# All row tiles of an attention block multiplied in pairs, with the steps of a batch written in a new order

## The chip, the cores and the metric

The kernel runs on one core of one Trainium2 chip. A core has a matrix engine (TensorE, in the profile PE, with its weight loads as PEld), three engines for elementwise work (VectorE or DVE, ScalarE or ACT, GpSimd or POOL) and SyncE (SP), which here only starts DMA transfers. Each engine runs its own list of instructions in the order in which the program wrote them, and waits where an instruction needs another engine's result. The metric is the time of one execution on the device in microseconds (us).

## The reference

The input x has 8 batches of 1024 rows by 256 columns, in float32. One block of a transformer is computed, with a modulation from a small vector c:

```python
mod = (_silu(L0_c) @ L0_wmod).reshape(L0_c.shape[0], 6, 1, -1)
sa, ca, ga, sb, cb, gb = (mod[:, 0], mod[:, 1], mod[:, 2], mod[:, 3], mod[:, 4], mod[:, 5])
...
h = _layernorm(x, axis=-1) * (1 + ca) + sa
x = x + ga * attn(h)      # scores (h*w_lhs)(h*w_rhs)^T, softmax over rows, times h
h = _layernorm(x, axis=-1) * (1 + cb) + sb
x = x + gb * ffn(h)       # relu(h W1 + b1) W2 + b2, inner width 1024
```

The gates ga and gb are first moved away from zero (at least 0.25 in size).

## The kernel before

**Tiles.** A batch has eight row tiles of 128 rows (NT = 8), in two halves g of four tiles (TH = 4, 512 rows). The main loop goes over batches b and tiles i; each pair (b, i) is a step. In step i of batch b the kernel computes the scores of tile i + 2 (`direct`, L412), works on the weights of tile i + 1 (called `late`), multiplies tile i's weights by the normalised x (`product`, `pair_begin`, `pair_end`), and does a part of the feed-forward work of batch b - 1. So attention of one batch runs beside the feed-forward part of the batch before. Batch 0 has no feed-forward part beside it and has its own loop body; `tail` (L1392) finishes the last batch's feed-forward work.

**Scores.** They are symmetric up to the column scales, so only columns at or right of the tile are computed; `mirror` (L433) transposes blocks on DVE, and `move` (L309) sends them through DRAM by SP (four writes D_m, one read) into the lower triangle. `row_max` (L469) takes a row's maximum on DVE, `max_turn` (L474) transposes it on PE into bank m, `subtract` (L479) and `exponent` (L491) make the weights pT.

**Products.** A full `product` (L501) is eight matmuls of 257 columns: 256 of x, scaled in the tile xg, and a column of ones that gives the sum. A pair of tiles can instead be multiplied by a scheme of seven half-size products (Strassen's, in Winograd's form) in place of eight. `pair_begin` (L547) makes two of them into the PSUM tile pp, ACT copies one to W, and `pair_begin_sum` (L566) adds them on DVE. `left_sums` (L575) makes four sums of weights on POOL; `right_sums` (L534) makes four of xg once per batch. `pair_end` (L587) makes the other five products into pq and pr, `pair_out` (L609) combines all on DVE and adds to x, `pair_stats` (L635) takes the statistics of the second layer norm. Before, tiles 0 and 5 use the full product and the pairs are (1,2), (3,4) and (6,7).

**Feed-forward.** It also uses seven products for eight. A step with i % 4 < 2 (`step_units`, L1186) does one unit of the first layer: products one and five (`unit_start`, L759, with the ACT copies k1 and k5), two, six (with the copy k2), three, seven and four (L774 to L821), in the banks A, B and E; relus follow on ACT, and `turn_first` and `turn_last` (L831, L839) make sums on POOL. Bank A takes products one, six, seven and four after one another, so each must wait until the result before it has been read. A step with i % 4 >= 2 (`step_rows`) does products of the second layer (`y_one` to `y_seven`, L850 to L887).  `y_gate` and `y_turn` scale the result and transpose it (T_y) through DRAM, `y_add` (L913) adds it to x on POOL and `y_out` writes x out.

**The next batch.** During batch b, each half of batch b + 1 goes through statistics (`prepare_stats`, DVE), `prepare_rstd` (ACT), `prepare_norm` (L281, four ACT instructions into xg), `prepare_blocks` (L340, transposes T_a on DVE, sent through DRAM to X_a), and `prepare_turn_apart` (L345), which scales X_a on ACT into the right and the left operand of the scores (two instructions each, L351). Additions and multiplications by rows (`x_plus`, `xg_times`) are put into a list, and `spare()` issues one of them on POOL at chosen places. The second layer norm goes through `ffn_rstd`, `ffn_norm`, `ffn_blocks` (T_f, X_f) and `ffn_turn` (hT on DVE and ACT, four sums hs on POOL).

**What sets the order.** The order is written out by hand, and `pin` (L72) holds every engine to it. Nothing is planned by costs. The step functions are the list of queues: a call writes its instructions into PE's, DVE's, ACT's, POOL's and SP's list at that place. PSUM has eight banks: two for scores (s), one each for m, A, B and E, two (o) for the products.

Of the kernel before, what the change touches and what calls it, by code (L numbers as in the profile page):

```python
# [24 lines left out]
def adaln_block_kernel(  # L25
# [158 lines left out]
    def columns(src, at):  # L184
        n = src.shape[0]
        pv = any_bank(f"pt_v{at}")
        nc.tensor.transpose(pv[:, :n], src, ident[:n, :n])
        nc.scalar.copy(cols[:, ds(at, n)], pv[:, :n])
# [398 lines left out]
    def pair_end(b, i, between=None):  # L587
# [5 lines left out]
        for n, (out, lhs, rhs) in enumerate((  # L593
# [6 lines left out]
            if between and n == 2:  # L600
                between()
# [385 lines left out]
    columns(wv, NI)  # L987
# [76 lines left out]
    def make_gcol():  # L1064
        pg = any_bank("pt_g")
        for j in range(2):
            for k in range(ND):
                nc.tensor.transpose(
                    pg[:, ts(j * ND + k, B)], rows_sb[:, 2 + j, ts(k, P)], ident[:B, :B]
                )  # L1070
        nc.scalar.copy(gcol.rearrange("p j k b -> p (j k b)"), pg[:, : 2 * ND * B])

# [32 lines left out]
    def make_columns():  # L1105
        make_gcol()
        columns(b1_rows, 0)
# [4 lines left out]
    def early(b, i):  # L1112

        if b == 0:

            if i in (1, 2):
                prepare_rstd(1, i - 1)
            elif i == 5:
                ffn_rstd(0, 0)
            if i in (1, 2):  # L1120
                prepare_norm(1, i - 1)
                x_plus(1, i - 1)
            if i in (3, 4):
                xg_times(1, i - 3)
            elif i == 5:
                prepare_turn(1, 0)
            elif i == 6:
                load_x(2, 0)
        else:
            if i == 2 and b + 1 < B:  # L1130
                prepare_norm(b + 1, 0)
            elif i == 6 and b + 2 < B:
                load_x(b + 2, 0)

    def turns(b, i):

        if b == 0 and i == 2:
# [4 lines left out]
        elif b == 0 and i == 3:  # L1142
            prepare_blocks(1, 1)
        if b > 0 and i == 2:
            ffn_turn(b - 1, 1)
        if i == (7 if b < B - 1 else 6):
            ffn_turn(b, 0)

    def middle(b, i):

        if i == 0:
            ffn_norm(b - 1, 1)
        elif i == (6 if b < B - 1 else 5):
            ffn_norm(b, 0)

    def norms(b, i):
        if b > 0 and i == 0:
            ffn_blocks(b - 1, 1)
        if b == 0:
            if i == 0:  # L1160
                prepare_start(1)
        elif b + 1 < B:
            if i == 1:
                prepare_start(b + 1)
                prepare_stats(b + 1, 0)
            elif i == 2:
                prepare_blocks(b + 1, 0)
                x_plus(b + 1, 0)
                xg_times(b + 1, 0)
        elif i == 5:  # L1170

            ffn_blocks(b, 0)
        if b == B - 1:
            return
        if i == 6:
            if b == 0:
                ffn_norm(b, 0)
            ffn_blocks(b, 0)
# [6 lines left out]

    def step_units(b, i, ahead, late, extra):  # L1186
        fb, fg, c = b - 1, i // TH, i % TH * 2
        ub, ug = (b - 1, 0) if i >= TH else (b - 2, 1)
        back = i % TH == 0 and ub >= 0
        more = b + 1 < B  # L1190
        main = {
            0: lambda n: product(b, 0, (n,)),
            1: lambda n: None,
            4: lambda n: None,
            5: lambda n: product(b, 5, (n,)),
        }[i]

        unit_start(fb, fg, c)
        if i == 0:
            ffn_rstd(b - 1, 1)  # L1200
        elif i == 4:
            y_gate(fb)
            if more:
                prepare_rstd(b + 1, 1)
        if ahead:
            mirror(*ahead)
        unit_two(c)
        if i == 4:
            y_turn(fb, 0)
        max_turn(*late)  # L1210
        unit_six(c)
        if i == 0 and back:
            for q in range(2):
                y_add(ub, ug, q)
        if i != 4:
            subtract(*late)
        if extra:
            exponent(*late)
        unit_three(c)
        if extra:  # L1220
            max_turn(*extra)
            unit_seven(c)
        if (b, i) == (B - 1, 5):
            ffn_rstd(b, 0)
        if i == 0 or (b, i) == (B - 1, 5):
            middle(b, i)
        if i == 1:
            exponent(*late)
            left_sum(b, i)
        elif i == 4 and more:  # L1230
            prepare_norm(b + 1, 1)
            x_plus(b + 1, 1)
        elif i == 5:
            exponent(*late)
            if more:
                prepare_turn_apart(b + 1, 1, 1)
        relu_left(c)
        if i == 0 and not extra:
            exponent(*late)
        if i == 1:  # L1240
            pair_begin(b, i, lambda: unit_seven(c))
        elif i == 4:
            pair_end(b, 3, lambda: unit_seven(c))
        else:
            main(0)
            if not extra:
                unit_seven(c)
            else:
                subtract(*extra)
        relu_right(c)  # L1250
        turn_first(c)
        if i == 5 and more:
            prepare_turn_apart(b + 1, 1, 0)
        if i == 4:
            if more:
                prepare_blocks(b + 1, 1)
                xg_times(b + 1, 1)
            weights(*late)
        main(1)
        unit_four(c)  # L1260
        if i == 1:
# [3 lines left out]
        if i == 4:  # L1265
            for q in range(2):
                y_add(ub, ug, q)
        if i in (0, 4):
            turn_last(c)
        turns(b, i)  # L1270
        norms(b, i)
        if extra:
            exponent(*extra)
        if i in (0, 5):
            product_out(b, i)
        elif i == 4:
            pair_out(b, 3)
            if b == B - 1:
                pair_stats(b, 3)
        if back:  # L1280
            y_out(ub, ug)

    def step_rows(b, i, ahead, late):
# [3 lines left out]
        if i == NT - 2:  # L1287
            for q in (1, 3):
                if (b, q) in two_t:
                    pair_stats(b, q)  # L1290
        if i == 2:
            left_sums(b, 1)
        if ending:
            pair_end(b, i - 1)
            pair_out(b, i - 1)
            pair_stats(b, i - 1)
        if i % TH == 2:
            if i == 6:
                max_turn(*late)
                weights(*late)  # L1300
                y_one(fb, fg)
            else:
                y_one(fb, fg)
                max_turn(*late)
            if ahead:
                mirror(*ahead)
            if i == 2:
                turn_last(2)
            y_two(fb, fg)
            if i == 2 and more:  # L1310
                prepare_rstd(b + 1, 0)
            elif i == 6 and more:
                ffn_rstd(b, 0)
            y_six()
            if i == 2:
                weights(*late)
            else:
                turn_last(2)
                pair_begin(b, i)
                left_sums(b, i)  # L1320
                pair_begin_sum(b, i)
        else:
            if i == 3:
                pair_begin(b, i, lambda: max_turn(*late))
            elif ahead:
                max_turn(*late)
            if ahead:
# [4 lines left out]
            if i == 3:  # L1332
                pair_begin_sum(b, i)
            if late:
                weights(*late)
            y_four(fb)
        spare()
        early(b, i)
# [205 lines left out]
```

## Time and profile before

| what | value |
|---|---|
| median of 3 runs | 780.77 us (780.23 to 780.78) |
| the profiled execution's own time | 780.81 us |
| its span in the profile | 779.0 us |
| DVE busy | 506.5 us (65%) |
| POOL busy | 473.7 us (61%) |
| ACT busy | 409.0 us (52%) |
| granted PE clock | full in all 40 slices |

A busy time is the time in which an engine executes instructions of the program; a matmul's end is modelled, so PE's starts tell more than its lengths. One `matmul` of the program in float32 makes two records, so a group of four matmuls shows as x8. A line of the timeline gives start, length, engine, the source line, the operation with output and input tiles, and in brackets the idle time before it and what ended it. Windows that are given without heading list the length, then busy time of PE, PEld, DVE, ACT and POOL with the number of instructions, the granted clock, the DMA share and GB/s.

### The profile page before, as it was taken

How to read it: one execution, taken by the hardware profiler on the slowest of the kernel's cores; microseconds unless marked ns; L12 is line 12 of the kernel's file. 1: busy time of each engine (PE TensorE's matmuls, PEld its weight loads, DVE VectorE, ACT ScalarE, POOL GpSimd, SP SyncE). 2: the span in 40 equal slices, each digit the busy share in tenths (PEclk: the TensorE clock that was granted, in tenths of full speed). 3: DMA queues.
4: the chain of work that ended last, by engine and by line, in shares of the span. 5: the costliest groups of instructions: out<-in, count | busy, mean ns of one | idle time of the engine just before them, and what ended most of it. 6: DMA issues, size and time to landing. Idle time of an engine off the chain costs nothing.

```text
span 779.0 us, 11552 instructions
## 1 busy us (share of the span) xinstructions
PE 757.4 (97%) x3876; PEld 624.4 (80%) x3876; DVE 506.5 (65%) x1075; ACT 409.0 (52%) x762; POOL 473.7 (61%) x481
## 2 busy tenths in 40 slices
PE   8999999999999999999999999999999999999998
PEld 4687788788987888778887888878888787988886
DVE  6787767576675767757667576766767576574421
ACT  4464637546474456645555455654637546262531
POOL 3753483866739577466766577566683866458320
PEclk9999999999999999999999999999999999999999
DMA  8033444265444543445533555335543354134220
GB/s 299 15 109 95 135 122 111 82 179 154 118 117 120 164 132 109 139 123 160 144 86 125 148 149 157 100 101 178 153 139 102 94 162 133 33 90 122 77 85 27
DMA packets 106210, 95.18 MB, mean 122 GB/s; under 512 B 29700, under 2 KB 98848, under 8 KB 106152
## 3 DMA queue, kind: packets, MB, share of 16 engines
q1 hardware_dynamic: 98408, 85.81, 38.2%
q10 hardware_dynamic: 7744, 8.65, 3.5%
q8 instruction: 30, 0.49, 0.3%
q14 instruction: 28, 0.23, 0.1%
HBM read 50.62 MB, written 43.81 MB: 121 GB/s over the span
## 4 chain that ended last, share of the span: by engine, by line
PE 76%; ACT 11%; DVE 6%; issue 5%; DMA 1%; DVEq 0%
PE psc L421 13%; PE pa L738 12%; PE ya L738 10%; PE po L509 9%; PE pe L738 6%; PE pr L603 5%; PE yc L738 5%; PE pp L557 4%; PE py L954 4%; PE pq L603 3%; PE pb L738 3%; ACT pT L492 2%; DVE pT L483 2%; PE yb L738 2%; ACT xg L290 2%
## 5 line engine op out<-in xcount | busy, mean ns | idle before, releaser
L421 PE MATMUL psc<-rT,lT 128*128 128x512 f32 (+3 forms) x384 | 134.7, 487 | 0.0
L421 PEld LDWEIGHTS psc<-rT,lT 128*128 128x128 f32 x384 | 68.2, 191 | 38.0 <-issue 27.0
L492 ACT ACTIVATE pT<-pT 128x1024 f32<-128x1024 f32 x64 | 67.7, 1058 | 58.1 <-DVE pT L483 58.1
L428 ACT COPY sc<-psc 128x512 f32<-128x512 f32 (+3 forms) x96 | 45.1, 476 | 90.7 <-PE psc L421 67.6
L483 DVE TENSOR_TENSOR pT<-sc,pm 128x1024 f32<-128x1024 f32 x64 | 77.3, 1207 | 9.4 <-PE pm L476 7.7
L509 PE MATMUL po<-xg,pT 128*128 128x257 f32 x352 | 82.9, 381 | 0.0
L836 POOL TENSOR_TENSOR ft<-f 128x512 f32<-128x512 f32 x28 | 35.7, 1274 | 74.4 <-ACT f L825 74.4
L471 DVE TENSOR_REDUCE m<-sc 128x1 f32<-128x1024 f32 x64 | 77.4, 1210 | 3.4 <-ACT sc L428 2.6
L738 PE MATMUL pa<-hT,w 128*128 128x256 f32 x256 | 67.5, 386 | 10.5 <-ACT f L817 9.9
L509 PEld LDWEIGHTS po<-xg,pT 128*128 128x128 f32 x352 | 66.3, 190 | 10.1 <-issue 0.7
L918 POOL TENSOR_TENSOR x<-x,Y 128x512 f32<-128x512 f32 x28 | 35.1, 1275 | 57.2 <-DMA Y<-D_y 57.2
L738 PEld LDWEIGHTS pa<-hT,w 128*128 128x128 f32 x256 | 46.8, 190 | 25.3 <-ACT f L817 13.4
L738 PE MATMUL pa<-hs,w1s 128*128 128x256 f32 x256 | 66.3, 381 | 0.1
L756 ACT COPY k<-pa 128x512 f32<-128x512 f32 x64 | 37.3, 583 | 47.7 <-PE pa L738 47.1
L444 DVE STREAM_TRANSPOSE Tm<-sc 128x896 f32<-128x896 f32 (+6 forms) x49 | 34.9, 711 | 32.1 <-ACT sc L428 31.8
L652 POOL TENSOR_TENSOR x<-x,rows 128x256 f32<-128x256 f32 x64 | 45.3, 740 | 14.7 <-ACT rows L1059 10.4
L738 PE MATMUL yc<-f,w2s 128*128 128x256 f32 x224 | 53.1, 380 | 0.9 <-DVE Y L877 0.9
L803 DVE SCALAR_TENSOR_TENSOR f<-pa,cols,k 128x256 f32<-128x256 f32 x64 | 28.0, 480 | 38.9 <-PE pa L738 38.9
L738 PE MATMUL ya<-ft,w 128*128 128x256 f32 x224 | 52.9, 380 | 0.0
L738 PEld LDWEIGHTS pa<-hs,w1s 128*128 128x128 f32 x256 | 45.4, 191 | 8.1 <-POOL pT L584 2.0
L573 POOL TENSOR_TENSOR s<-pT 128x512 f32<-128x512 f32 x21 | 26.7, 1273 | 40.9 <-ACT pT L492 36.5
L724 POOL TENSOR_TENSOR hs<-hT 128x256 f32<-128x256 f32 x16 | 11.6, 725 | 60.5 <-DVE hT L715 60.5
(161 smaller groups left out, 1743.9 us busy)
## 6 DMA issues: line engine op xcount, KB each, us to landing
D_f<-T_f SPq DMA_DIRECT2D x60, 128.0 KB, 2.4
X_f<-D_f SPq DMA_DIRECT2D x15, 512.0 KB, 3.9
D_a<-T_a SPq DMA_DIRECT2D x56, 128.0 KB, 2.3
D_y<-T_y SPq DMA_DIRECT2D x56, 128.0 KB, 3.2
Y<-D_y SPq DMA_DIRECT2D x14, 512.0 KB, 3.6
out_dram<-x SPq DMA_DIRECT2D x14, 512.0 KB, 4.0
X_a<-D_a SPq DMA_DIRECT2D x13, 512.0 KB, 3.4
x<-in_L_attn_x_dram ACTq DMA_DIRECT2D x12, 512.0 KB, 4.1
```

The lines of the kernel that those rows point to most:

```text
L421: nc.tensor.matmul(psc[:, : hi - lo], lhsT=lT_t[b, i // TH][:, k, ts(i % TH, P)], rhs=rT_t[b, n][:, k, lo - n * HALF : HALF], start=(k == ...
L428: nc.scalar.copy(score_row(b, i)[:, lo // V : hi // V, :], psc[:, : hi - lo].rearrange("p (n v) -> p n v", v=V),)
L471: nc.vector.tensor_reduce(m, score_row(b, i), AX.XY, ALU.max)
L483: nc.vector.tensor_tensor(pT.rearrange("p j (a v) -> p j a v", v=V), score_columns(b, i), pm[:, :P].rearrange("p (j a v) -> p j a v", j=1, ...
L492: nc.scalar.activation(pT_t[b, i], pT_t[b, i], AF.Exp)
L509: nc.tensor.matmul(po[:, : D + 1], lhsT=pT[:, t, :], rhs=xg_t[b][:, t, 0 : D + 1], start=(t == 0), stop=(t == NT - 1),)
L603: nc.tensor.matmul(out, lhsT=lhs[:, t, :], rhs=rhs[:, t, :], start=(t == 0), stop=(t == TH - 1),)
L652: queue.append(lambda: nc.gpsimd.tensor_tensor(out, in0, row, op))
L738: nc.tensor.matmul(out, lhsT=lhsT, rhs=rhs, start=first, stop=True, skip_group_check=True)
L756: nc.scalar.copy(k, src)
L836: add(ft[:, 0, c : c + 2], f22, f12, ALU.subtract)
L918: nc.gpsimd.tensor_tensor(x2, x2, y, ALU.add)
```

## The change

From batch 1 on every tile is in a pair: (0,1), (2,3), (4,5), (6,7). `pair_begin` is called in the even steps, `pair_end` in the odd ones. In steps 0, 1, 4 and 5 products of the unit stand between pair products: in an even step products seven and three stand between the two of `pair_begin`; in an odd step they stand after the first product of `pair_end`, and product four after the third. In steps 2 and 6 a y product stands between the two of `pair_begin`. Product four's relu is on DVE in steps 0 and 4 (with the exception of batch 1's step 0).

The steps are written in a new order. Among what moves: T_f of `ffn_blocks(b-1, 1)` from step 0 to 1; the load of the next batch's second half from step 2 to 1; the normalisation, T_a and additions of the next batch's second half from step 4 to 3, with `prepare_norm` between the two `prepare_turn_apart` of the first half; in step 2 the statistics of the pair and `ffn_turn` stand ahead of `row_max`; in step 7 `row_max` stands behind `y_turn` and `ffn_turn`; in step 6 `row_max` stands behind `ffn_norm`. In batch 0 only a helper changes: small columns are transposed into a bank that another transpose already uses.

```diff
-    def columns(src, at):
+    def columns(src, at, pv):
         n = src.shape[0]
-        pv = any_bank(f"pt_v{at}")
...
-            if between and n == 2:
-                between()
+            if n in between:
+                between[n]()
...
+        def sums():
+            unit_seven(c)
+            unit_three(c)
...
         max_turn(*late)
         unit_six(c)
+        subtract(*late)
         if i == 4:
             y_turn(fb, 0)
...
+        def after():
+            exponent(*late)
+            relu_left(c)
+            relu_right(c)
+            turn_first(c)
...
+        elif even:
+            pair_begin(b, i, sums)
             exponent(*late)
+            left_sums(b, i)
+            relu_left(c)
+            if i == 0:
+                ffn_norm(b - 1, 1)
+            relu_right(c)
+            turn_first(c)
+            unit_four(c, True)
+        elif i == 1:
+            pair_end(b, i - 1, {1: sums, 3: lambda: (after(), unit_four(c))})
+            if more:
+                prepare_start(b + 1)
+                prepare_stats(b + 1, 0)
+        else:
...
+            spares(4)
+            pair_end(b, i - 1, {1: sums, 3: lambda: (after(), unit_four(c))})
             if more:
                 prepare_turn_apart(b + 1, 1, 1)
+                prepare_turn_apart(b + 1, 1, 0)
...
+        if even:
             pair_begin_sum(b, i)
         if ahead and ahead != extra:
             row_max(*ahead)
...
         if i == 2:
+            y_one(fb, fg)
+            max_turn(*late)
+            turn_last(2)
+            mirror(*ahead)
+            y_two(fb, fg)
+            subtract(*late)
+            if more:
+                prepare_rstd(b + 1, 0)
+            y_six()
+            exponent(*late)
+            pair_begin(b, i, y_seven)
+            left_sums(b, i)
+            if more:
+                prepare_norm(b + 1, 0)
+                x_plus(b + 1, 0)
+            pair_begin_sum(b, i)
+            pair_stats(b, 0)
+            ffn_turn(b - 1, 1)
+            row_max(*ahead)
+            if more:
+                prepare_blocks(b + 1, 0)
+                xg_times(b + 1, 0)
+                prepare_stats(b + 1, 1)
+        elif i == 6:
+            max_turn(*late)
+            subtract(*late)
+            y_one(fb, fg)
+            exponent(*late)
+            turn_last(2)
             if ahead:
                 mirror(*ahead)
             y_two(fb, fg)
+            pair_begin(b, i, y_six)
+            left_sums(b, i)
+            y_seven()
+            pair_begin_sum(b, i)
+            pair_stats(b, 4)
+            if more:
                 ffn_rstd(b, 0)
+                ffn_norm(b, 0)
+                row_max(*ahead)
+                ffn_blocks(b, 0)
...
+        elif i == 3:
+            max_turn(*late)
+            mirror(*ahead)
+            y_five(fb, fg)
+            subtract(*late)
+            if more:
+                prepare_rstd(b + 1, 1)
+            exponent(*late)
+            y_four(fb)
+            y_three()
+            if more:
+                prepare_turn_apart(b + 1, 0, 1)
+                prepare_norm(b + 1, 1)
+                prepare_turn_apart(b + 1, 0, 0)
+            spares(8)
+            row_max(*ahead)
+            pair_end(b, 2)
+            if more:
+                x_plus(b + 1, 1)
+                prepare_blocks(b + 1, 1)
+                xg_times(b + 1, 1)
+            pair_out(b, 2)
...
+            if ahead:
+                pair_end(b, i - 1)
+                y_turn(fb, fg, True)
+                ffn_turn(b, 0)
+                spares(8)
+                row_max(*ahead)
+                pair_out(b, i - 1)
```

## The prediction

> **What bounds the kernel now.** I read the busy shares first, then one batch period, then PE's timeline inside it, then the queues that feed PE.
>
> ```profile
> PE 757.4 (97%) x3876; PEld 624.4 (80%) x3876; DVE 506.5 (65%) x1075; ACT 409.0 (52%) x762; POOL 473.7 (61%) x481
> ```
>
> PE is the bound, but a busy PE here includes modelled ends, so I take its work from starts. Two stretches from one second-unit start of step 5 to the next (length; busy PE, PEld, DVE, ACT, POOL; clock):
>
> ```profile
> 131.93:225.47 93.54, 91.47 (x481) 76.61 (x481) 62.98 (x135) 52.26 (x99) 62.15 (x61) 1.00 0.47 133
> 225.47:319.02 93.55, 91.59 (x481) 76.50 (x481) 63.09 (x134) 52.24 (x98) 62.15 (x61) 1.00 0.46 133
> ```
>
> A batch takes 93.55 us and repeats exactly, at full clock. PE's timeline, from step 4's end on:
>
> ```profile
> 222.43 1.03 PE L738 MATMUL pa<-hT,w 128*128 128x256 f32 x4
> 223.29 0.61 PE L421 MATMUL psc<-rT,lT 128*128 128x128 f32 x4
> 225.47 1.13 PE L738 MATMUL pa<-hT,w 128*128 128x256 f32 x4 [1.57 <-ACT f L817]
> ...
> 232.60 1.90 PE L509 MATMUL po<-xg,pT 128*128 128x257 f32 x8
> 234.33 1.03 PE L738 MATMUL pa<-hT,w 128*128 128x256 f32 x4
> ...
> 242.65 2.00 PE L738 MATMUL ya<-ft,w2s 128*128 128x256 f32 x8 [0.29 <-ACT Y L855]
> ...
> 256.30 1.05 PE L603 MATMUL pr<-tsum,s 128*128 128x128 f32 x8
> 257.19 1.06 PE L603 MATMUL pq<-tsum,pT 128*128 128x128 f32 x8
> ```
>
> Starts give the prices: half a full product 1.73 (232.60 to 234.33), a half-size product 0.89, a unit's product 0.865, one of a y product 1.73, scores 1.72 per 512 columns (1.29 for 384, 0.87, 0.45), a maximum's transpose 0.11. With these PE's work is 90.5 per batch, so only 3.05 are waits: 1.73 at 223.74 (bank A is freed by ACT's relu L817, late behind an exponent), 0.45 at 242.2, 0.25 at 282.3 (DVE L803), 0.17 at 215.1, and about 0.1 of slow restart after each.
>
> The queues that matter for the new order, from three engines' timelines:
>
> ```profile
> 246.47 0.27 ACT L563 COPY W<-pp 128x129 f32<-128x129 f32 x1 [1.41 <-PE pp L557]
> ...
> 293.21 2.06 ACT L290 ACTIVATE xg<-x,rs,ra 128x256 f32<-128x256 f32 x4
> ```
> ```profile
> 246.77 0.29 DVE L569 TENSOR_TENSOR W<-pp,W 128x129 f32<-128x129 f32 x1 [3.71 <-ACT W L563]
> ...
> 295.30 1.30 DVE L331 STREAM_TRANSPOSE T_a<-xg 128x512 f32<-128x512 f32 x2 [1.26 <-ACT xg L290]
> ```
> ```profile
> 296.63 1.76 SPq L315 DMA_DIRECT2D D_a<-T_a  x4
> 300.41 0.34 SPq L318 DMA_DIRECT2D X_a<-D_a  x1
> ```
> ```profile
> X_a<-D_a SPq DMA_DIRECT2D x13, 512.0 KB, 3.4
> ```
>
> W is copied only after the second half of the pair's first products (ends 246.26). The transposed next batch travels through DRAM: T_a ends 296.60, the read is issued 3.8 later and lands 3.4 after that, 7.2 in all.
>
> **PE's work.** Two full products (4 x 1.73 = 6.92) become a fourth pair (7 x 0.89 = 6.23): -0.69, work 89.8 per batch. The Trainium skill, Perfetto Trace Analysis, section Optimizing Tensor Performance, says that larger matmuls are more efficient than smaller; here 257 columns cost 0.216 a record and 128 cost 0.111, so halving costs 3% and the eighth saved becomes a tenth. Without that 3% the saving would be 0.87 and the forecast 1 us lower.
>
> By step the work is 10.53, 12.80, 10.53, 11.05, 8.81, 11.07, 12.25, 12.77 (steps 0 to 7).
>
> **The fourth pair elsewhere.** POOL gets four sums more (4 x 1.27 = 5.1; 62 to 67 of 94), DVE about 1.9 (3.1 for sum and outputs against 2 x 0.64), ACT 0.27. The second relu of steps 0 and 4 moves to DVE (L815, no row of that form; nearest L861 0.43 and L803 0.48; I take 0.85 for two, between 0.7 and 0.95). None is a bound by its total.
>
> **Waits removed.** 1.73, 0.45, 0.25 and 0.17 have their causes moved: the relu is no longer behind an exponent, the half products stand between y products and between a unit's. k2's copy (0.2 + 0.58) now has one half product (0.89) as cover: just enough.
>
> **Waits added.** I walked each engine's queue in program order; latencies by the rows: 0.2 from PE to DVE or ACT, 0.05 otherwise. Let P be PE's end of step 2, the second half of pair 2's first products.
> - DVE now has, behind P: W copy (ACT) 0.5, sum 0.22, statistics of tiles 0 and 1 1.1, hT (L715) 0.5, only then the maximum of row 4, 1.13: ready P+3.5. Step 3 has nothing ahead of that maximum's transpose but 1.29 of scores. PE waits 2.2 where it waits 0 now; y_five and y_four queue behind it.
> - T_a of the next batch's first half comes next and ends at P+4.7, where before it stood 2 us ahead of P's place. X_a lands at P+11.9. ACT's own queue (exponent, gated copy) is done at P+10.2, so it waits there. Behind it on ACT: the right half (1.4), the four norms of the second half (2.1), the left half (1.4), and then step 4's score copy and k1.
> - DVE waits for these norms (P+15.4) with T_a of the second half (1.22), and queued behind that are pair_out of pair 2 (2.6), a mirror 0.3, L780 0.8, a subtract 1.13, T_y 1.22, L803 0.88: P+23.7. The last product of step 4's unit waits for L803, takes 0.97 after the restart, L815 frees bank A at P+25.75, and step 5's first unit starts at P+25.8. By work alone it would be 11.05 + 8.81 + 0.45 = P+20.3. So 5.5, with a restart 5.6, of wait per batch. PE's own path through k1 (P+18.0) would give P+25.0, so DVE's part of it is 0.8.
> - Step 1: ACT carries W, exponent, relu, four norms, relu from step 0 (from 9.87 to 14.5 after that step's start), then two score copies and k1, done at 15.8; PE wants it at 15.4: 0.5 (0 to 1.0).
> - Moved and covered: the maxima of steps 5 and 7, after T_y and hT, are used 5 us later; ffn_norm and its T_f in step 6 come 1.4 later, and hT is ready when step 0 wants it, 2.6 into it. POOL's four sums in step 0 delay turn_first to 19.2, needed at 29 in step 2. The x additions in step 5 stand behind eight POOL instructions and end at P+43; y_one's copy wants that buffer at P+42 and y_six that copy at P+44: 1 us of cover, below. SP: y_out, the Y read and x loads keep their order to the moves; read-backs wait for nothing new; a mirror's move behind X_a's read in step 3 lands 5 us before its subtract.
>
> Unknown above all is X_a's way: 3.7 to 5.1 to the issue in the eight cases seen and 2.3 to 6.4 to landing over all reads of that line, so 6.0 to 10.2 about 7.2, the common case. Each us is one us per batch; below 5.5 ACT's queue takes over. The skill, DMA: Bandwidth & Descriptors, section Rules for kernel authors, says to issue a DMA early and wait for it late, so that its fixed cost is covered; in the trace ACT comes to X_a 8.4 after T_a's end (296.60 to 305.04) and finds it landed, while the new order puts T_a late and its reader soon. Were the rule still kept, ACT's own queue would set the start and the forecast would be 786.
>
> **Sum.** Period 89.8 + 5.6 + 0.5 = 95.9, +2.35. Six batches (1 to 6) have the next batch to prepare: +14.1. Batch 1 starts with a second exponent, W and two relus in ACT's step 0, k1 of step 1 about 1.2 later: +1.2. Batch 7 lacks the preparation; it loses its waits of 2.5 and 0.7 of work, and keeps 2.3 (maximum), 0.8 (bank A in step 5) and 0.5: +0.3. Batch 0: a copy of small columns shares a bank, so PE's 0.85 before pmc can go: -0.5 (0 to -0.85). Together +15.1 on the profiled execution's 780.81 (span 779.0 and 1.8 around it; the median shown is 780.77): 796.
>
> **Rivals.**
> - Not slower: W's sum is let go by the first half product, 2.6 before P (y_seven and the second half lie between). Then the whole chain moves 2.6, the maximum is in time and the period is 93.3: 780, no change; from 2.5 on it decides. Against it: L569 reads the second half, and 246.47 comes after it.
> - POOL becomes the bound in steps 5 and 6: if its additions slip by more than 1 us, y_six waits. A slip of 2.5 (two instructions more ahead of it) gives 1.5 x 6 = 9: 805. For it: POOL's longest queue is there; against: it is idle a third of the time.
> - The transposed half is in time for ACT's queue (P+10.2): 1.7 x 6 less, 786. Then DVE and k1 still hold PE.
> - All new waits covered by something I do not see: 90.3 per batch, about 760.
>
> **How the numbers follow.** My sum 0.60, the early transposed half 0.14, POOL 0.12, early release 0.08, all covered 0.06. Noise of this kernel is about 0.2%. Faster 0.09 (covered, and half of the early release's scatter), same 0.04, slower 0.87. Range 783 to 806: from below the early-landing case to POOL's, leaving out the covered and the released case and the longest landings.
>
> **What the profile after would show.** Period near 96; L603 and L557 counts up by a third, L509 only batch 0's 128 records; PE waiting at the maximum's transpose in step 3 (DVE L471, some 2.2, seven times); DVE T_a idle for ACT's norms; ACT L351 idle for the DMA of X_a; the L817 wait of 1.6 gone, in its place DVE L803 and L815 at bank A. I am wrong if T_a or the maximum stand earlier in DVE's queue than I read, or if X_a lands in under 5.5.

## The result and the profile after

The changed kernel takes 802.10 us (median of four runs, 800.52 to 805.40), the kernel before 780.77 beside it. The ratio is 1.028, with a 95% interval of 1.0242 to 1.0318: slower, by about 21 us. The profiled execution took 800.52 us with a span of 798.5, so against the profiled execution of before (780.81) there are 19.7 us to explain.

First the busy times on the page of the kernel after.

```profile
PE 761.0 (95%) x4044; PEld 628.3 (79%) x4044; DVE 530.6 (66%) x1136; ACT 400.6 (50%) x743; POOL 507.7 (64%) x509
```

PE has hardly more to do than before, and no other engine came near its limit: POOL went from 61% to 64%. The time went into gaps on PE. The next lines are two batch periods of the kernel after, counted from P, the start of step 3's scores, to the next P (length; busy PE, PEld, DVE, ACT, POOL; granted clock, DMA share, GB/s).

```profile
204.14:300.13 95.99, 91.73 (x506) 76.78 (x505) 66.66 (x143) 50.82 (x94) 66.99 (x66) 1.00 0.47 129
300.13:396.60 96.47, 91.73 (x506) 76.78 (x505) 66.09 (x143) 50.79 (x94) 67.06 (x66) 1.00 0.46 129
```

The six periods from P = 108.55 to 685.38 have a mean of 96.14 ((685.38 - 108.55) / 6) where before had 93.55: 6 x 2.59 = 15.5 of the 19.7. Where a period loses them is seen on PE's timeline behind P = 204.14.

```profile
204.14 1.46 PE L420 MATMUL psc<-rT,lT 128*128 128x384 f32 x4
207.74 0.29 PE L475 MATMUL pm<-ident,m 128*128 128x128 f32 x1 [2.15 <-DVE m L470]
...
211.75 1.99 PE L737 MATMUL yc<-f,w2s 128*128 128x256 f32 x8 [0.26 <-DVE Y L876]
...
221.98 1.10 PE L737 MATMUL pa<-hs,w1s 128*128 128x256 f32 x4 [0.21 <-ACT k L755]
...
227.86 1.10 PE L737 MATMUL pa<-hT,w 128*128 128x256 f32 x4 [0.92 <-DVE f L802]
...
229.93 1.13 PE L737 MATMUL pa<-hT,w 128*128 128x256 f32 x4 [0.53 <-DVE f L814]
```

Step 5's first unit starts at 229.93, that is P+25.79; by work alone it would be P+20.3. The wait is paid in pieces, 2.15 at the maximum first, and 0.92 and 0.53 at bank A last. What stands behind the pieces is one chain. DVE's timeline of the kernel after:

```profile
206.39 1.20 DVE L470 TENSOR_REDUCE m<-sc 128x1 f32<-128x1024 f32 x1
207.52 1.29 DVE L330 STREAM_TRANSPOSE T_a<-xg 128x512 f32<-128x512 f32 x2
...
219.72 1.30 DVE L330 STREAM_TRANSPOSE T_a<-xg 128x512 f32<-128x512 f32 x2 [4.01 <-ACT xg L289]
...
226.88 0.83 DVE L802 SCALAR_TENSOR_TENSOR f<-pa,cols,k 128x256 f32<-128x256 f32 x2
```

The transposed half goes through DRAM by SP:

```profile
208.83 1.75 SPq L314 DMA_DIRECT2D D_a<-T_a  x4
212.64 0.34 SPq L317 DMA_DIRECT2D X_a<-D_a  x1
```

And ACT, which waits for it and has the next half's norms queued behind:

```profile
216.21 1.52 ACT L350 ACTIVATE rT<-X_a,sides 128x512 f32<-128x512 f32 x2 [1.85 <-DMA X_a<-D_a]
217.63 2.06 ACT L289 ACTIVATE xg<-x,rs,ra 128x256 f32<-128x256 f32 x4
```

Read together: T_a ends at P+4.7, the read is issued 3.8 later (212.64), ACT gets the data at P+12.07, norms the second half until P+15.55, DVE has stood 4.01 for that, and the product that PE needs (L802) comes from DVE's queue at P+22.7 to P+23.6. The other periods show the same chain with another arrival of X_a, here the earliest and the latest of the six:

```profile
120.21 1.52 ACT L350 ACTIVATE rT<-X_a,sides 128x512 f32<-128x512 f32 x2 [1.43 <-DMA X_a<-D_a]
505.13 1.52 ACT L350 ACTIVATE rT<-X_a,sides 128x512 f32<-128x512 f32 x2 [2.45 <-DMA X_a<-D_a]
```

These are P+11.66 and P+12.68 (P = 108.55 and 492.45), and the periods are 95.59 and 96.61: as much as X_a is later, the period is longer. The largest of PE's waits of the kernel after (us in total, times, longest):

```profile
PE pm L475 <- DVE m L470: 15.0, 7, 2.2
PE pa L737 <- DVE f L802: 4.9, 6, 0.9
PE pa L737 <- DVE f L814: 3.7, 7, 0.5
PE yc L737 <- DVE Y L876: 3.2, 6, 1.9
PE pa L737 <- ACT k L755: 2.7, 4, 1.0
```

The wait of 1.6 for the relu on ACT (L817, seven times before) is gone, as the change's parts would have it.

The other 4.2 us lie outside these periods. The first P comes 1.2 earlier than before, and from the last P to the end it takes 113.1 in place of 107.9, of which 1.0 is more work. There PE waits 1.91 for y_five's sum, which before it waited 0.89 for, and then runs slowly:

```profile
738.81 2.71 PE L737 MATMUL yc<-f,w2s 128*128 128x256 f32 x8 [1.91 <-DVE Y L876]
```
```profile
722.70 1.29 DVE L330 STREAM_TRANSPOSE T_f<-X_f 128x512 f32<-128x512 f32 x2
...
733.55 0.55 DVE L714 TENSOR_SCALAR hT<-X_f,modT 128x512 f32<-128x512 f32 x1 [4.59 <-DMA X_f<-D_f]
...
738.35 0.40 DVE L876 TENSOR_TENSOR Y<-yc,Y 128x256 f32<-128x256 f32 x1
```

In the kernel before, these are:

```profile
701.37 1.29 DVE L331 STREAM_TRANSPOSE T_f<-X_f 128x512 f32<-128x512 f32 x2
...
711.02 0.93 DVE L715 TENSOR_SCALAR hT<-X_f,modT 128x512 f32<-128x512 f32 x1
```

In both kernels hT stands in step 6 of the last batch. Before, DVE came to it 8.4 us after the end of T_f and found X_f there. In the new order T_f stands behind the pair_out of tiles 4 and 5, and DVE comes to hT 5.0 after its end, while X_f takes 9.6. DVE idles 4.59 there for this DMA, and pair_out, the statistics and y_five's sum (L876) are queued behind it.

The granted clock was the surprise. These are stretches of 2 us of the kernel after, behind one of the waits of 2.15, and one behind the wait of 1.91 (same columns as above):

```profile
594.00:596.00 2.00, 2.00 (x6) 1.55 (x6) 1.84 (x9) 0.13 (x1) 1.92 (x3) 0.50 0.62 138
...
740.00:742.00 2.00, 2.00 (x6) 1.61 (x5) 0.45 (x2) 0.00 (x0) 2.00 (x4) 0.50 0.00 0
```

Here the clock is half. On PE's timeline of the kernel after, the same place as in the period shown above, four batches later:

```profile
592.66 0.29 PE L475 MATMUL pm<-ident,m 128*128 128x128 f32 x1 [2.15 <-DVE m L470]
592.79 3.25 PE L737 MATMUL yc<-f,w2s 128*128 128x256 f32 x8
595.83 2.27 PE L737 MATMUL ya<-ft,w 128*128 128x256 f32 x8
597.93 1.89 PE L737 MATMUL yc<-f,w2s 128*128 128x256 f32 x8
```

From start to start y_five takes 3.04 and y_four 2.10, where each takes 1.73 at full clock: 1.68 lost, which is about 3.4 us at half speed. I call this a dip. The same wait of 2.15 behind P = 204.14 was followed by none.

### The profile page after: what moved, and what is told of

The parts are those of the page before. It is cut to its first block, busy times and chain, and to the rows that moved or that the text cites. A ratio compares the mean times of both kernels' runs of the same rounds, so it can differ in the third digit from the quotient of the medians.

```text
span 798.5 us, 12066 instructions
## 1 busy us (share of the span) xinstructions
PE 761.0 (95%) x4044; PEld 628.3 (79%) x4044; DVE 530.6 (66%) x1136; ACT 400.6 (50%) x743; POOL 507.7 (64%) x509
## 4 chain that ended last, share of the span: by engine, by line
PE 69%; DVE 12%; ACT 7%; DMA 7%; issue 2%; SPq 1%; POOL 1%; ACTq 0%; DVEq 0%; POOLq 0%
PE pa L737 11%; PE psc L420 11%; PE ya L737 10%; PE pr L602 7%; PE pe L737 5%; PE pp L556 5%; PE pq L602 4%; PE po L508 3%; PE py L953 3%; PE yc L737 3%; PE yb L737 3%; DMA X_a<-D_a 2%; PE pb L737 2%; ACT X_f L667 2%; DMA D_a<-T_a 2%
## 5 line engine op out<-in xcount | busy, mean ns | idle before, releaser
L572 POOL TENSOR_TENSOR s<-pT 128x512 f32<-128x512 f32 x28 | 35.5, 1268 | 128.0 <-ACT pT L491 111.4
L420 PEld LDWEIGHTS psc<-rT,lT 128*128 128x128 f32 x384 | 66.0, 191 | 36.7 <-issue 25.6
L427 ACT COPY sc<-psc 128x512 f32<-128x512 f32 (+3 forms) x96 | 43.3, 471 | 73.7 <-PE psc L420 55.4
L737 PE MATMUL pa<-hs,w1s 128*128 128x256 f32 x256 | 69.3, 393 | 4.0 <-ACT k L755 2.7
L556 PEld LDWEIGHTS pp<-xg,pT 128*128 128x128 f32 x448 | 58.7, 191 | 3.1 <-ACT pT L491 0.3
L556 PE MATMUL pp<-xg,pT 128*128 128x129 f32 x448 | 59.2, 275 | 0.0
L602 PE MATMUL pq<-tsum,pT 128*128 128x128 f32 (+1 forms) x448 | 59.1, 275 | 0.0
L737 PE MATMUL yc<-f,w2s 128*128 128x256 f32 x224 | 55.6, 393 | 3.2 <-DVE Y L876 3.2
L602 PEld LDWEIGHTS pq<-tsum,pT 128*128 128x128 f32 x448 | 56.7, 192 | 1.4
```

Source lines behind the costliest of these rows:

```text
L420: nc.tensor.matmul(psc[:, : hi - lo], lhsT=lT_t[b, i // TH][:, k, ts(i % TH, P)], rhs=rT_t[b, n][:, k, lo - n * HALF : HALF], start=(k == ...
L427: nc.scalar.copy(score_row(b, i)[:, lo // V : hi // V, :], psc[:, : hi - lo].rearrange("p (n v) -> p n v", v=V),)
L556: nc.tensor.matmul(out, lhsT=lhs[:, t, :], rhs=xg_t[b][:, h * TH + t, P : P + XS], start=(t == 0), stop=(t == TH - 1),)
L572: nc.gpsimd.tensor_tensor(s1, *halves(pT_t[b, i + 1]), ALU.add)
L602: nc.tensor.matmul(out, lhsT=lhs[:, t, :], rhs=rhs[:, t, :], start=(t == 0), stop=(t == TH - 1),)
L737: nc.tensor.matmul(out, lhsT=lhsT, rhs=rhs, start=first, stop=True, skip_group_check=True)
```

## The experiments

Theory: four pairs cost nothing; the order does, through the chain above (maximum late, T_a late, X_a, norms, DVE's queue, bank A). First rival: PE's largest named wait, 15.0 us at the maximum, is the loss, and goes with its cause. Second: a fourth pair is too much for POOL, DVE or ACT. Third, once the dips were seen: the clock takes the time. Line numbers of the changed kernel and of its variants are the same but for small shifts. The kernel before took 780.5 to 781.2 us beside each group of runs. Periods are between P's, as above.

### The maximum right behind the pair's sum

```diff
             pair_begin_sum(b, i)
+            row_max(*ahead)
             pair_stats(b, 0)
             ffn_turn(b - 1, 1)
-            row_max(*ahead)
```

> Edit: in step 2 the maximum of row 4 moves to the place right behind the pair's sum, ahead of the statistics and hT. Chain theory: the maximum is ready 1.6 us sooner, so PE's wait at its transpose falls from 2.15 to about 0.5, but everything that DVE does up to the last of these instructions ends at the same moment; the wait comes back at y_three, which then waits for DVE L876 (0.26 in the changed kernel, about 1.9 here), the period stays at 96.0 and the time at 799 to 803. Rival 'the named wait is the cost': 1.65 x 7 = 11.6 less, about 790. Rival 'load' (the fourth pair's own work on DVE and POOL is the cost): no change either, but then the wait does not come back at y_three.

Measured: 797.60 us (796.57 to 799.36), ratio 1.0217 (1.0199 to 1.0235), a little below the 799 to 803 expected. PE's two largest waits in this variant:

```profile
PE yc L737 <- DVE Y L876: 13.4, 7, 2.0
PE pm L475 <- DVE m L470: 4.3, 7, 0.6
```

The maximum is 1.5 earlier, its wait fell from 2.15 to 0.6, and the mean period stayed at 96.1 ((685.30 - 108.67) / 6). The wait came back at y_three, two products later: it needs y_five's sum, which stands on DVE behind the same instructions in all, T_a and the statistics among them. The rival is out for these periods: the largest wait of the list was where PE met the chain, not what made it long. The 4.5 us by which the time is below 802.1 come from the last batch, which has no next one to prepare: from the last P to the end it takes 109.2 in place of 113.1 in the profiled executions, since the wait at the maximum is 1.5 shorter, that for y_five's sum is 1.19 in place of 1.91, and no dip (a stretch of half clock, see above) follows it.

### The maximum ahead of the pair's first products

```diff
             exponent(*late)
+            row_max(*ahead)
             pair_begin(b, i, y_seven)
...
             ffn_turn(b - 1, 1)
-            row_max(*ahead)
```

> Edit: the maximum of row 4 moves ahead of the pair's first products in step 2, where DVE idles. Chain theory: PE's wait of 2.15 at its transpose goes, DVE's chain behind P loses one instruction of 1.13, so X_a, ACT, DVE and bank A come 1.1 sooner: the period falls by 1.1 to 94.9, y_three waits about 1.4 for L876; batch 7, which has no next batch, gains 2.2. Together 9 less, and the clock returns to 1.00 for about 1 to 3 more: 789 to 793. Rival 'named wait': 2.15 x 7 = 15 and the clock, 784 to 786. Rival 'load': 799 to 803.

Measured: 790.58 us (789.71 to 791.15), ratio 1.0124 (1.0109 to 1.0139), mean period 94.9 ((677.84 - 108.46) / 6). Here the maximum runs while DVE would wait for W, so everything behind it on DVE comes earlier: T_a ends at P+3.8 in place of P+4.7. X_a is scaled from P+11.0 on average in place of P+12.1, 0.9 by the move and the rest because its way was a little shorter in this run; together that is the 1.2 that the period gained. The first move only swapped DVE's work around; this one took 0.9 us out of the chain.

### The second half's norms ahead of both scalings

```diff
             if more:
-                prepare_turn_apart(b + 1, 0, 1)
                 prepare_norm(b + 1, 1)
+                prepare_turn_apart(b + 1, 0, 1)
                 prepare_turn_apart(b + 1, 0, 0)
```

> Edit: in step 3 the normalisation of the next batch's second half moves ahead of the two scalings of X_a on ACT; nothing else changes, the work is the same. Chain theory: the normalisation runs while the transposed half is still in flight, DVE's transpose T_a of the second half starts near P+12.5 in place of P+15.5, pair_out and the unit's additions behind it no longer hold bank A; step 5's first unit starts near P+23.8 in place of P+25.8 (P is PE's end of step 2). The period falls by 2.0 to 94.0 and the time by 12, to 788 to 791. Rivals 'load' and 'named wait': the wait of 2.15 at the maximum stays and so does the time, 799 to 803.

Measured: 792.62 us (792.33 to 794.30), ratio 1.0156 (1.0140 to 1.0172), above the 788 to 791 expected. Three periods of this variant:

```profile
299.56:394.83 95.27, 92.46 (x507) 77.93 (x506) 66.97 (x143) 51.20 (x94) 66.97 (x66) 0.98 0.45 130
394.83:488.94 94.11, 91.05 (x507) 76.69 (x506) 66.51 (x143) 51.28 (x94) 66.99 (x66) 1.00 0.46 132
488.94:583.04 94.10, 91.03 (x506) 76.68 (x505) 66.66 (x143) 51.17 (x94) 66.99 (x66) 1.00 0.45 132
```

At full clock the period is 94.1: the wait for the transposed half no longer holds the norms, and 2.0 of the loss per batch is gone. ACT now comes to X_a when it has landed, so its scatter is out of the period too. Four of the six periods are 95.3, each with a dip behind the wait of 2.15 at the maximum. In the changed kernel the chain hid most of a dip (its period with one is 96.32, only 0.5 more than X_a's arrival at P+11.88 gives it by the relation above); here, with the chain shorter, it shows. That raised the question of what the clock took altogether.

### The gaps filled

Two unread products of 512 columns, ahead of the maximum's transpose in step 3 of batches 1 to 7, and ahead of y_three in the last step:

```diff
+    def fill(name, n=2):
+        pf = bank("m", f"fill_{name}")
+        for _ in range(n):
+            nc.tensor.matmul(pf, lhsT=ident, rhs=w1[:, 0, 0:HALF], start=True, stop=True)
...
         elif i == 3:
+            fill(f"{b}_3")
             max_turn(*late)
...
+            if ending:
+                fill("end")
             y_three()
```

> Edit: two matmuls of 512 columns whose result nobody reads are put ahead of the maximum's transpose in step 3 of each batch from 1 on, and ahead of the last y_three of the second-layer products in the last step, so that PE has 1.7 us of other work in its longest waits. Clock theory (a part of the loss and the scatter of the changed kernel, 800.5 to 805.4 at mean clocks of 0.995 to 0.992, comes from PE idling over 1.9 us at a time, after which the granted clock is low for some microseconds): the period stays at 96.0, the clock returns to 1.00 and all runs lie within 0.5 us of each other near 798 to 799. If the clock has nothing to do with these waits: the same scatter and the same clock, 800 to 805.

Measured: 796.92 us (795.43 to 797.46), ratio 1.0202 (1.0183 to 1.0221), clock 1.000 throughout, mean period 95.86 ((683.88 - 108.74) / 6). The products do no useful work and shorten no chain, yet the time falls by 5.2 from 802.1. I had expected 798 to 799. Not all of the 5.2 is shown to be the clock. Between the two profiled executions the difference is 3.6: 2.1 behind the last P, where the dip of 1.7 is gone, and 1.7 in the six periods, of which one dip makes about 0.5 and the rest is X_a, scaled from P+11.9 on average in place of P+12.1. The slower executions of the changed kernel have lower mean clocks (0.993 at 803.6, 0.992 at 805.4, against 0.995 at 800.5), which fits more dips, but they have no trace. The rest of the loss, 16 us, stays at full clock, so the clock is not the main cause.

The same filling with the norms ahead of both scalings:

> The changed kernel with the norms ahead of both scalings in step 3 (as in the earlier run of that name) and two unread products of 512 columns ahead of the maximum's transpose in step 3 of batches 1 to 7 and two ahead of y_three in the last step; nothing reads them. Clock theory: all six periods are 94.1 to 94.3, where that run had four of 95.3 at a clock of 0.98; 4 x 1.15 and some in the last batch go: 786 to 789 us. Rival (the longer periods of that run had another cause, and the clock only shows it): the time stays within 1.5 of that run's 792.6.

Measured: 786.42 us (786.26 to 786.63), ratio 1.0069 (1.0054 to 1.0084). All six periods are 94.13, two of them here:

```profile
108.99:203.12 94.13, 92.76 (x510) 77.45 (x509) 67.51 (x143) 51.26 (x94) 67.00 (x66) 1.00 0.46 132
203.12:297.25 94.13, 92.77 (x511) 77.46 (x509) 66.59 (x143) 51.28 (x94) 67.04 (x66) 1.00 0.47 132
```

So the periods of 95.3 were the clock, and adding idle products to this variant made it 6.2 us faster.

### T_a early

```diff
             exponent(*late)
+            if more:
+                prepare_norm(b + 1, 0)
             pair_begin(b, i, y_seven)
             left_sums(b, i)
             if more:
-                prepare_norm(b + 1, 0)
+                prepare_blocks(b + 1, 0)
                 x_plus(b + 1, 0)
...
             if more:
-                prepare_blocks(b + 1, 0)
                 xg_times(b + 1, 0)
```

> Edit of the changed kernel: in step 2 the normalisation of the next batch's first half moves ahead of the pair's first products and its transpose T_a ahead of the pair's sum on DVE; the maximum stays where it is and so comes 0.7 later. Chain theory: X_a is asked for 3.3 sooner and ACT's own queue sets the start of its scaling (P+9.9 in place of P+12.1); bank A follows, period 94.1 where the clock holds, although PE's wait at the maximum GROWS from 2.15 to 2.9; that longer wait lowers the clock after it, 1.2 us per batch where it does: 788 to 797. Rival 'named wait': 0.7 x 7 = 5 more than the changed kernel, 802 to 807.

Measured: 804.84 us (804.45 to 807.54), ratio 1.0319 (1.0300 to 1.0337). Missed: it is no faster at all, although no wait for L802 is left. PE's timeline of this variant behind P = 205.54, and its clock:

```profile
210.49 0.45 PE L475 MATMUL pm<-ident,m 128*128 128x128 f32 x1 [3.50 <-DVE m L470]
210.73 3.62 PE L737 MATMUL yc<-f,w2s 128*128 128x256 f32 x8
214.15 2.96 PE L737 MATMUL ya<-ft,w 128*128 128x256 f32 x8
216.94 1.89 PE L737 MATMUL yc<-f,w2s 128*128 128x256 f32 x8
```
```profile
205.54:303.32 97.78, 93.64 (x506) 78.82 (x505) 67.45 (x143) 51.35 (x95) 66.87 (x66) 0.97 0.44 127
303.32:399.93 96.61, 92.46 (x507) 77.93 (x506) 67.61 (x143) 51.12 (x95) 66.88 (x66) 0.98 0.45 129
```

T_a now stands ahead of the maximum on DVE, and the wait for the maximum grew from 2.15 to 3.50. Each of the six is followed by a dip. In the first period shown y_five and y_four take 3.42 and 2.79, so 2.75 more than 2 x 1.73; in the second (3.36 and 1.78) the loss is 1.68. Without the dips the two would be 95.03 and 94.93. Whether that reading is right, the next variant tells: four unread products in step 3 and two in the last step, on top of the early T_a.

> The changed kernel with the norms and T_a of the next batch's first half early in step 2 (as in the run before it of that name), and besides four unread products of 512 columns into bank m ahead of the maximum's transpose in step 3 of batches 1 to 7, and two ahead of y_three in the last step; nothing reads them. They fill most of the 3.5 us in which PE stood idle there (two of them took 1.7 in the earlier filling). Clock theory (the early T_a did remove the wait for the transposed half, and what made that kernel no faster was the low clock after the longer wait, 2.75 per batch on y_five and y_four): the mean clock comes to 0.99 or more, y_five and y_four take 1.73 each, and the period goes from 96.6 to 97.8 down to about 94.2: 783 to 789 us. Rival (the period is set by another chain through step 5, the clock is a symptom): the period stays at 96 or above, the wait appears at bank A in step 5, 797 to 805.

Measured: 793.02 us (792.78 to 793.24), ratio 1.0154 (1.0137 to 1.0171), clock 1.000.

```profile
203.65:298.62 94.97, 94.22 (x515) 78.31 (x514) 67.85 (x143) 51.30 (x95) 66.98 (x66) 1.00 0.45 131
298.62:393.57 94.95, 94.21 (x514) 78.29 (x513) 67.90 (x143) 51.31 (x95) 66.94 (x66) 1.00 0.46 131
```

The period is 94.95, what the one before gives without its dips, and 11.8 us are gone by keeping PE busy. The number I had expected (94.2 and 783 to 789) was too low by 0.75 per batch: PE stands 3.7 at the maximum whether it is idle or filled, and I had not counted that. Early T_a is worth about 0.9 per batch against the filled kernel (95.86), not more, since it pushes the maximum back.

### All of the chain early

The maximum ahead of `pair_begin`, the norms ahead of both scalings, and the second half's statistics and `prepare_rstd` moved back in step 3, so that y_five's sum and the subtract come earlier on DVE:

```diff
             exponent(*late)
+            row_max(*ahead)
             pair_begin(b, i, y_seven)
...
-            row_max(*ahead)
...
-                prepare_stats(b + 1, 1)
...
             if more:
-                prepare_rstd(b + 1, 1)
+                prepare_stats(b + 1, 1)
             exponent(*late)
             y_four(fb)
+            if more:
+                prepare_rstd(b + 1, 1)
             y_three()
             if more:
-                prepare_turn_apart(b + 1, 0, 1)
                 prepare_norm(b + 1, 1)
+                prepare_turn_apart(b + 1, 0, 1)
                 prepare_turn_apart(b + 1, 0, 0)
```

> Edit of the changed kernel: the normalisation of the second half ahead of the scalings of X_a in step 3, the maximum of row 4 ahead of the pair's first products in step 2, and the statistics of the second half moved from the end of step 2 behind step 3's subtraction. The same work, four pairs. Chain theory: no wait over 0.7 us is left in steps 3 and 4 (k1 0.2, k2 0.4, bank A behind L815 0.7); the period falls to 91.6, the clock stays at 1.00, the time is 768 (764 to 773), below the kernel before. Rival 'load' (four pairs put too much on DVE and POOL): at or above the 780 of the kernel before.

Measured: 772.56 us (771.76 to 773.42), ratio 0.9898 (0.9882 to 0.9915): faster than both kernels, with all four pairs in it. PE's largest waits from the first P on, and one period of this variant:

```profile
PE pa L737 <- DVE f L814: 3.7, 7, 0.5
PE yc L737 <- DVE Y L876: 2.6, 1, 2.6
```
```profile
292.32:384.00 91.68, 90.96 (x506) 76.88 (x505) 66.88 (x143) 51.02 (x94) 66.92 (x66) 1.00 0.47 136
```

The mean period is 91.8 ((659.29 - 108.73) / 6). Separately the two moves gave 1.2 and 2.0 per batch; together with the statistics' move, 4.3. POOL has 66.9 of 91.7 to do: the second rival is out.

### Tiles 0 and 1 as full products

The variant before, but from batch 2 on tiles 0 and 1 use the full product, so three pairs as in the kernel before:

```diff
         elif even:
-            pair_begin(b, i, sums)
...
+            if i == 0 and b > 1:
+                product(b, i, (0,))
+                sums()
+                product(b, i, (1,))
...
         elif i == 1:
-            pair_end(b, i - 1, {1: sums, 3: lambda: (after(), unit_four(c))})
+            if b > 1:
+                product(b, i, (0,))
+                sums()
+                after()
+                unit_four(c)
+                product(b, i, (1,))
...
```

> Edit: the kernel of the order just described, but tiles 0 and 1 go back to full products from batch 2 on (no pair sums, no four sums on POOL for them, statistics with each tile). This prices the fourth pair by itself. By PE's work 0.69 x 6 = 4.1 more than with four pairs; the shorter chain of DVE behind the pair of tiles 2 and 3 (1.1 of statistics less) can give back up to 0.5 a batch: 1 to 4 above the four-pair kernel of this order. Rival 'load': below it.

Measured: 775.31 us (774.12 to 775.88), ratio 0.9931 (0.9916 to 0.9946): 2.75 more than with the fourth pair, as expected, but as a balance of unlike parts. In four of the six periods it takes 0.4 to 0.6 more (92.14 against 91.74 in the first), where the work alone says 0.69. In the two others it takes 2.1 and 2.5 more (93.76 and 94.25): X_a came late there (scaled from P+12.25 and P+12.87, else from P+10.8 to P+11.1), and PE waits 1.29 and 1.90 in step 4 for k1, queued behind it on ACT. Behind the last P it takes 2.9 less (108.5 against 111.4), for its wait for y_five's sum is 1.29 without a dip where the four-pair variant waits 2.64 and has one. So by the four undisturbed periods the fourth pair gains about 0.5 per batch in a good order.

### The relu alone, in the kernel before

```diff
-        unit_four(c)
+        unit_four(c, i == 4)
```

> Edit of the kernel before, nothing of the change but one part: the relu of product four goes to DVE in step 4. Chain theory: bank A in step 5 is freed after DVE's subtract and two relus, 0.65 after PE's scores in place of 1.73: 1.07 x 7 = 7.5 less, 773 (772 to 776). So the removed wait was real and the changed kernel had this gain inside its loss. If the wait only moves to the next instruction (k2, L780): 780.

Measured: 777.49 us (776.99 to 777.95), ratio 0.9961 (0.9946 to 0.9976): less gain than the 772 to 776 expected. The wait at bank A goes from 1.57 to 0.55, and four of the six periods are 92.40, 1.15 shorter, near the 1.07 expected (the others 92.48 and 92.76). Over the six that is 6.5 (6 x 93.55 less 554.84), but the time gained is 3.2. The rest was given back in the last batch, where the wait before y_one became longer:

```profile
699.10 3.11 PE L738 MATMUL ya<-f,w 128*128 128x256 f32 x8 [2.94 <-ACT f L817]
702.01 2.50 PE L738 MATMUL yb<-f,w 128*128 128x256 f32 x8
```

Before, this wait was 1.12 and at full clock. Now y_one and y_two take 2.91 and 2.33 from start to start, 1.78 more than 2 x 1.73: 1.8 of wait and 1.8 of dip.

## Why the prediction was right or wrong

The forecast was 796.0 (783 to 806), slower. The result lies inside, on the right side, 6.1 above the number.

- **PE's work, 89.8 per batch:** holds. In the period from 204.14 the 5.49 behind P leave 90.5 of 95.99, which is this work and 0.7 that it does not explain, small waits and restarts. "Repeats exactly" was said of the two periods of before that are shown; the six from P to P vary from 93.42 to 93.80, with a mean of 93.57.
- **The maximum, P+3.5, wait 2.2:** measured P+3.6 and 2.15, seven times.
- **The transposed half, P+11.9:** measured P+12.07 in the period shown, P+11.66 to P+12.68 over the six, 12.13 on average. X_a's way took 7.4 in the one shown, where 7.2 was taken from the profile of before. Norms end at P+15.55, against P+15.4. That each us of X_a's way is one us per batch holds: 95.59 with P+11.66, 95.99 with P+12.07, 96.61 with P+12.68.
- **Bank A and step 5, P+25.8:** measured P+25.79, in the pieces 2.15, 0.26, 0.21, 0.92 and 0.53 with a slow restart after each. These waits come to 4.07; the rest of the 5.49 is in the restarts and in the modelled ends from which a wait is counted. Over the six batches it is P+25.4 to P+26.4, with X_a. The two variants that take the maximum or the norms out of the chain shortened the period by about what the chain says of each, and the one that only reorders did not, so this is shown and not only argued.
- **Step 1, 0.5 (0 to 1.0):** k1's copy is late by some 0.3 there (an idle time of 0.12 and a slow restart, six times); within the bounds. The longer waits for k1, 0.21, 0.67 and 0.82, stand in step 4, longest in the batches in which X_a lands latest; the 1.0 of the list is ahead of the first P.
- **k2's cover "just enough":** not quite. Step 4's product behind the half product starts 0.24 late and restarts slowly.
- **Waits removed:** the relu's wait and the others of before are gone.
- **Sum of the six periods, +14.1:** measured +15.5 (15.4 against the mean of 93.57), and +13.9 with the gaps filled (6 x (95.86 - 93.55)). The mechanism was right: with X_a at P+11.9 the measured periods would be 95.8, where the sum said 95.9. The difference is mainly the size of one term, X_a's way, which was 0.23 a batch longer on average, and one dip of about 0.5. That the filled kernel comes so near is the full clock and a shorter way of X_a in that run (P+11.9 on average).
- **Batches 0 and 1, +0.7 together:** not seen. The first P comes 1.2 earlier than in the kernel before (108.55 against 109.76), and the new order puts 1.0 more of PE's work behind P (from the last P on, five more half products, 4.45, in place of a full product's 3.46), so these two batches cost about nothing.
- **Batch 7, "+0.3": this step failed.** "It loses its waits of 2.5" was wrong for one of them: y_five's sum, 0.89 before, became 1.91, since hT in step 6 now waits 4.59 for X_f with that sum queued behind it. I had followed hT in the middle batches only. A wait of 1.91 instead of none and the dip of 1.7 behind it are 3.6 that the sum did not have, the largest part of what was missing.
- **The clock: not in the sum at all.** All 40 slices of before show full clock with waits of up to 1.58, and I priced a wait as its own length and a restart of 0.1. The filled kernel is 5.2 below the median, and some 2.2 of the 3.6 between the profiled executions are dips (1.7 in the last batch, about 0.5 in the periods). How much of the 6.1 that the forecast was short is clock in the executions without a trace stays open. That the filled kernel's 796.9 is so near 796.0 is partly luck: the wait of the last step is also in it.
- **The rivals:** the early release did not come (the maximum waited as foreseen); POOL did not become the bound; the transposed half was not in time for ACT's queue, which waited 1.43 to 2.45 for it (1.7 foreseen).

## What to carry to other kernels

A wait list names the place where the bound engine meets a chain of in-order queues, not the link to move: before an edit, follow each engine's queue in program order from the moved instruction to the next product that needs it, and move the link that has slack behind it. A transfer through memory with 7 us between its start and its reader belongs early, and nothing that others need should be queued behind its reader. A wait of 2 us or more on TensorE can cost more than its length, since the clock may fall behind it. The first and last pass of a loop are to be followed on their own.

## What the runs showed of the hardware

TensorE's granted clock falls to half after a wait of some 2 us, and not after each. The profiled runs of before, of the changed kernel and of seven variants without filling (the maximum in both places, the norms first, T_a early, all early, the full products, the relu alone) give, by length of PE's wait:

| wait, us | waits | followed by a dip |
|---|---|---|
| 1.57 to 1.71 (before; maximum early) | 12 | 0 |
| 1.90 to 2.17 | 23 | 9 |
| 2.53 to 2.68 | 3 | 2 |
| 2.94 to 3.50 | 7 | 7 |

A dip costs PE 1.6 to 1.8 us, and 2.8 in three of the waits of 3.50, where the clock stays low twice as long. The Trainium skill, TensorE: Matmul & The Clock Gate, Part 1, says that the clock gate looks at activity in a free-running window of about 3.4 us and halves the clock after an idle window. The duration seen here, about 3.4 us at half speed for a loss of 1.7, agrees with that window. The length of gap does not: the page, in its section Why this matters for your kernels, warns of gaps above about 3 us, and here 9 of 23 gaps of 1.90 to 2.17 were enough.

The clock of these executions shows what decides. Within a run every fall and rise lies on one fixed grid of 3.413 us; in the kernel after, the two stretches of half clock begin 146.77 apart, 43 steps:

```profile
593.17:596.58 3.41, 3.41 (x10) 2.71 (x9) 3.25 (x12) 0.50 (x2) 3.33 (x6) 0.50 0.54 135
739.94:743.35 3.41, 3.41 (x9) 2.72 (x9) 0.67 (x2) 0.91 (x3) 3.41 (x6) 0.50 0.01 2
```

The seven executions with dips have 38 waits of the table. Cut at the run's own grid, all 17 waits that have 2.03 us or more within one stretch of the grid are followed by half clock in the next stretch, none of the 18 that have 1.88 or less is, and of the three between (1.91, 1.91 and 1.98) one is. So how a wait lies to the grid decides which of such similar waits are followed by a dip, and a stretch need not be idle throughout. The spread of the changed kernel, 800.5 to 805.4, would fit this, but only one of its executions has a trace.
